# A decoder layer's attention: the second copy of each projection from the first, one division for both heads of a pair, and the transpose by features moved in the slot

## The chip, the core and the metric

The kernel runs on one core of a Trainium2 chip. The core has a matrix engine (TensorE; PE in the profile, its weight loads PEld), VectorE (DVE), ScalarE (ACT), GpSimd (POOL) and SyncE (SP), which here only issues DMAs. The engines run side by side, each through its own queue of instructions in order, and wait for one another by semaphores. Products land in PSUM, which has eight banks of 128 x 512 fp32; everything else lies in SBUF.

The metric is the time of one execution on the device in microseconds. Lower is better.

## What is computed

One pre-norm decoder layer on x (4 batches, 1024 rows, 256 features), with 16 heads of 16 features:

```python
x = x + self_attention(layernorm(x))            # windows of 128 rows, each with the window before it, causal
x = x + cross_attention(layernorm(x), ctx)      # 77 keys, a mask over them, biases on q, k, v and the output
x = x + ffn(layernorm(x))                       # fake-quantised, silu(gate) * up, 704 inner features
```

In both attentions a head's output is `softmax(q k^T / 4) v`, with q, k and v from projections of 256 by 256, and the heads' outputs go through one more projection. The change touches how q and k are laid out and how the softmax's division and the turn of its result are done.

## The kernel before

**Stages.** After the loads and the first normalisation comes the attention of all batches in one long loop, and then the feed-forward part. The mask's rows are compared on the device; here they are alike, so `attention(True)` runs, in which `alike` is true and `queue_of[0]` is SyncE's DMA queue.

**Jobs, units, slots.** The attention has eight jobs in this order: S0, S1, S2, X0, S3, X1, X2, X3 (S self, X cross, and the batch). The 16 heads are in two groups g of eight. A group's projection gives 128 rows: four slots of 32 rows (j), each with two heads of 16 features, parity o = 0 and o = 1. Scores are taken for all j of one (job, g, o) at once, each j in its own strip of 32 rows of TensorE. A unit is (job, g, o, u); u goes over four quarters of the rows in S and two halves in X. There are 96 units, and slots go over them in order. In a slot, work is issued in this order, for every engine alike:

1. the values of a half that has come ready: `weighted_values`, `normalise`, `by_features` (L1239 to L1243; later in the last job's tail);
2. tasks by due time, among them `project` (q or k, by halves of the rows), `values`, `normed_T`, `out_project` and the preparation of the weights; then lighter work beside (statistics, quantisation);
3. `put_maxima`, if a (job, g, o) has all its maxima;
4. `maxima` of the unit five slots ahead (`LEAD` = 5): score products sc_n with queries on the partitions, and on VectorE the row maxima out of PSUM, with the causal mask added (L757) or without (L768);
5. `weights` of this unit: score products sc_t with keys on the partitions, and ScalarE's exp (L822, L844), in S also GpSimd's causal select (L826).

**How one head of two is picked.** `project` (L344) makes both heads' rows of a group in one bank ps_p, and ScalarE reads that bank twice, once for each parity, into two tiles q[g, 0] and q[g, 1] (or k): with `rows[o]`, a column of ones and zeros, as scale, the other head's 16 rows become zero. Of these zero rows one carries the softmax's shift: `put_maxima` (L776) turns the maxima by TensorE, ScalarE copies them (mxT), and four DMAs of SyncE write their negatives into row (1 - o) * 16 of every slot of q; k has a one in that row, from the bias `onerow[o]` (L369). Thus sc_t comes out with the maximum subtracted. In X one more row carries the mask: kx has the mask's row there and q a one, by the bias tile bq_p (`nextrow`, L363). q[g, o] and k[g, o] are eight buffers in turn (`qks`).

**Banks.** All PSUM tiles are whole banks of one pool of eight, given out in turn. A slot takes four for sc_n, four for sc_t and one for every task or value in it. A bank can be written again once the engine that reads it has.

**After the weights.** `weighted_values` (L847) multiplies the weights with the values for one (job, g, o, half) into ps_av, the sum of the weights beside them in column 16; VectorE transposes the bank by blocks of 32 (L880) into o_sb. `normalise` (L882) takes the reciprocal of the sums (L888) and multiplies (L890) into aN, one parity at a time. With o = 1 done, `by_features` (L897) transposes aN back (L902) into aT, from which `out_project` (L904) reads. A half's `out_project` may start in the slot after its last values (`task(end, ...)`, L1201).

Of the kernel before, what the change touches and what calls it, by code (L numbers as in the profile page):

```python
# [25 lines left out]
def decoder_layer(  # L26
# [175 lines left out]
    with ExitStack() as att:  # L202
# [13 lines left out]

        rows, qrows, onerow, nextrow = [], [], [], []
        for o in range(NS):
# [3 lines left out]
            for dst, first, n in (  # L222
# [15 lines left out]
                nc.vector.tensor_reduce(dst, at, AX.XY, ALU.max)  # L238
            q = wp.tile([P, 1], F32, name=f"qrows{o}")
            nc.vector.tensor_scalar(q, m, QSCALE, None, ALU.mult)  # L240
            rows.append(m)
            qrows.append(q)
            onerow.append(w)
            nextrow.append(n2)


        f = stage.tile([P, P], F32, name="cb_f", tag="stage")
        nc.gpsimd.memset(f, 0.0)
# [35 lines left out]
        class Job:  # L284


            def __init__(self, kind, b):
                self.kind, self.b = kind, b
                self.leads = (kind, b) == ("S", 0)
                self.st = {}  # L290
                self.xn, self.xnT, self.vs, self.q, self.k = {}, {}, {}, {}, {}
                self.aN, self.aT, self.mx, self.pts, self.av = {}, {}, {}, {}, {}

            def branch(self):
# [49 lines left out]
        def project(job, g, which, hf):  # L344

            out = job.q if which == "q" else job.k
            w = job.wq if job.kind == "X" else (wq_s if which == "q" else wk_s)
            if hf == 0:
                for o in range(NS):
                    out[g, o] = next_of("qk", qks)  # L350
            ps = bank("ps_p")
            for c in range(NC):
                by_columns(
                    ps,
                    w[:, c, g * P : (g + 1) * P],
                    job.xnT[hf][:, c, :],
                    start=(c == 0),
                    stop=(c == NC - 1),
                )
            for o in range(NS):  # L360
                dst = out[g, o][:, hf * HS : (hf + 1) * HS]
                if job.kind == "X":
                    nc.scalar.activation(  # L363
                        dst, ps, AF.Identity, bias=job.bq[:, g, o : o + 1], scale=qrows[o]
                    )
                elif which == "q":
                    nc.scalar.activation(dst, ps, AF.Copy, scale=qrows[o])  # L367
                else:
                    nc.scalar.activation(dst, ps, AF.Identity, bias=onerow[o], scale=rows[o])  # L369

# [41 lines left out]
        def attention(alike):  # L412
# [16 lines left out]
            vx = wp.tile([SK, B, H + 1, HD + 1], F32, name="vx")  # L429
            bq_p = wp.tile([P, NP, NS], F32, name="bq_p")  # L430
            bk_p = wp.tile([P, NP, NS], F32, name="bk_p")
# [7 lines left out]
            def prep_cross():  # L439
# [12 lines left out]
                def biases():  # L452
                    for name, dst, by, plus in (("q", bq_p, qrows, nextrow), ("k", bk_p, rows, onerow)):
                        for o in range(NS):
                            nc.vector.tensor_scalar(dst[:, :, o], raws[name], by[o], None, ALU.mult)
                            nc.vector.tensor_scalar(
                                dst[:, :, o], dst[:, :, o], plus[o], None, ALU.add
                            )

# [256 lines left out]
            def maxima(job, g, o, u):  # L716
# [33 lines left out]
                for j in range(NJ):  # L750
                    if job.kind == "S":

                        for i in range(2):
                            t = 2 * u + i
                            n = 2 * P if t else P
                            junk = work.tile([P, 2 * P], BF16, name="junk", tag="junk", bufs=2)
                            nc.vector.tensor_tensor_reduce(  # L757
# [18 lines left out]
            def put_maxima(job, g, o):  # L776
# [5 lines left out]
                mxT = work.tile([NJ * NT, P], F32, name="mxT", tag="mxT", bufs=2)  # L782
                nc.scalar.copy(mxT, ps[: NJ * NT, :P])
                for j in range(NJ):
                    row = j * SL + (1 - o) * HD
# [15 lines left out]
            def weights(job, g, o, u):  # L801
# [34 lines left out]
                else:  # L836
# [5 lines left out]
                    for j in range(NJ):  # L842
                        pt = work.tile([SK, HS], F32, name="ptx", tag="pt", bufs=16)
                        nc.scalar.activation(pt, banks[j][:SK], AF.Exp)  # L844
                        job.pts[g, o, j, u] = pt

            def weighted_values(job, g, o, hf):  # L847
                ps = bank("ps_av")
# [25 lines left out]
                if job is jobs[-1] and (g, o, hf) == (NP - 1, NS - 1, NH - 1):  # L874
                    job.av[g, o, hf] = next_of("xnT", xnTs)[
                        :, 0, :
                    ]
                else:
                    job.av[g, o, hf] = work.tile([P, HS], F32, name="o_sb", tag="o_sb", bufs=1)
                nc.vector.transpose(job.av[g, o, hf], ps)  # L880

            def normalise(job, g, o, hf, tail):  # L882

                if o == 0:
                    job.aN[g, hf] = work.tile([P, HS], F32, name="aN", tag="aN", bufs=2)
                on = job.av[g, o, hf].rearrange("p (s e) -> p s e", e=SL)
# [5 lines left out]
                    on[:, :, 0:HD],  # L892
                    rec.to_broadcast([P, HS // SL, HD]),
                    ALU.mult,
                )
# [320 lines left out]
            for slot in range(first, last):  # L1216
# [21 lines left out]
                else:  # L1238
                    for args in values_of.get(slot, ()):  # L1239
                        weighted_values(*args)  # L1240
                        normalise(*args, tail)
                        if not tail:
# [25 lines left out]
                if now:  # L1268
                    if alike or not (ahead and now[0].kind == "X"):
                        weight_bias(*now)  # L1270
                    weights(*now)
                for fn, args in late.get(slot, ()):
                    fn(*args)
# [321 lines left out]
```

## Time and profile before

| | us |
|---|---|
| median of three runs (663.86 to 665.63) | 664.09 |
| the profiled execution, whole | 664.85 |
| its span, first to last instruction | 663.1 |
| attention loop in that span, about | 30 to 545 |
| TensorE, VectorE, ScalarE, GpSimd busy | 613.6, 542.9, 367.9, 269.7 |

The granted TensorE clock averages 0.990 over the span. The page of the profile gives busy time by engine, the chain of work that ended last, and the costliest groups of instructions; a group's line reads: source line, engine, operation, what it writes <- what it reads, shapes, count | busy us, mean ns of one | idle time of the engine before it and what ended it. A timeline row is start, length, engine, line, operation and count, and in brackets the idle time before it. Where ScalarE reads a bank twice in a row, one timeline row with x2 holds both.

### The profile page before, as it was taken

The numbers are of one execution on the slowest core, as the hardware profiler recorded it, in microseconds if no ns is written. First come the engines' busy times: TensorE is split into PE (matmuls) and PEld (weight loads), VectorE is DVE, ScalarE is ACT, GpSimd is POOL, SyncE is SP. The second block draws the span as 40 slices with busy tenths as digits, with TensorE's granted clock in tenths as the row PEclk, the third lists the DMA queues.
The fourth block names the chain that finished last, engine by engine and source line by source line (L and its number), as shares of the span: only waits on it lengthen the run. The fifth ranks groups of instructions, "written<-read, shape, count | busy, mean of one in ns | idle before, by whom it ended". The sixth has DMA issues, their size and how long they took to land.

```text
span 663.1 us, 20225 instructions
## 1 busy us (share of the span) xinstructions
PE 613.6 (93%) x7862; PEld 350.8 (53%) x7862; DVE 542.9 (82%) x1922; ACT 367.9 (55%) x672; POOL 269.7 (41%) x520
## 2 busy tenths in 40 slices
PE   9899899999999999999999999999999997887775
PEld 6456565566555665654456656544444345333564
DVE  6878878768779799678997997897878787789896
ACT  2365564644555534655564456447465565788392
POOL 3164533637234567640054878436601141111032
PEclk9999999999999999999999999999999999989899
DMA  8100100000000000000000000000000110000057
GB/s 290 48 4 15 38 3 3 19 4 6 17 28 11 11 10 11 13 11 19 3 10 11 12 24 26 4 3 4 3 2 4 38 62 17 1 0 1 1 95 164
DMA packets 18078, 17.42 MB, mean 26 GB/s; under 512 B 2998, under 2 KB 17335, under 8 KB 17975
## 3 DMA queue, kind: packets, MB, share of 16 engines
q1 hardware_dynamic: 15783, 14.21, 6.7%
q0 software_dynamic: 1904, 1.84, 2.2%
q8 instruction: 64, 1.05, 0.6%
q14 instruction: 39, 0.32, 0.1%
q10 hardware_dynamic: 288, 0.00, 0.0%
HBM read 9.47 MB, written 6.03 MB: 23 GB/s over the span
## 4 chain that ended last, share of the span: by engine, by line
PE 61%; DVE 26%; ACT 6%; issue 5%; POOL 1%; DVEq 0%; ACTq 0%
PE ps_p L304 13%; PE ps_av L856 7%; PE sc_t L812 7%; PE sc_n L727 6%; PE ps_op L304 6%; PE ps_av L866 4%; DVE junk L757 4%; PE sc_t L841 3%; PE ps_v L304 3%; PE sc_n L742 3%; DVE bnst L192 2%; DVE o_sb L880 2%; PE pg L1393 2%; ACT shared L369 2%; PE ps_idle L117 2%
## 5 line engine op out<-in xcount | busy, mean ns | idle before, releaser
L757 DVE CUSTOM_DVE_ANT_0 junk<-sc_n,cboth 128x256 bf16<-128x256 f32 (+1 forms) x512 | 172.3, 403 | 35.1 <-PE sc_n L727 35.0
L822 ACT ACTIVATE pt<-sc_t 128x512 f32<-128x512 f32 (+1 forms) x256 | 125.4, 576 | 84.9 <-PE sc_t L812 84.9
L826 POOL TENSOR_SCALAR_AFFINE_SELECT pt<-pt 128x256 f32<-128x256 f32 x256 | 102.6, 409 | 114.9 <-ACT pt L822 104.7
L812 PE MATMUL sc_t<-shared 32*128 32x256 f32 (+1 forms) x1024 | 87.1, 375 | 1.4 <-DVE vx L532 0.3
L844 ACT ACTIVATE ptx<-sc_t 77x512 f32<-77x512 f32 x128 | 65.3, 597 | 37.0 <-PE sc_t L841 37.0
L727 PE MATMUL sc_n<-shared 32*128 32x256 f32 (+1 forms) x1024 | 73.6, 387 | 2.9 <-ACT shared L369 1.6
L812 PEld LDWEIGHTS sc_t<-shared 32*128 32x128 f32 x1024 | 65.0, 184 | 13.6 <-ACT shared L367 3.2
L320 POOL TENSOR_SCALAR xn<-x,mv,rs 128x256 f32<-128x256 f32 x56 | 69.9, 1254 | 0.0
L160 POOL TENSOR_SCALAR ve<-mv 128x4 f32<-128x4 f32 x20 | 4.7, 234 | 153.3 <-DVE mv L194 153.2
L880 DVE STREAM_TRANSPOSE o_sb<-ps_av 128x512 f32<-128x512 f32 x63 | 45.0, 714 | 23.8 <-PE ps_av L856 13.7
L304 PE MATMUL ps_p<-shared,w_s 128*32 128x512 f32 x512 | 60.9, 595 | 3.0 <-DVE mx L757 1.4
L727 PEld LDWEIGHTS sc_n<-shared 32*128 32x128 f32 x1024 | 45.7, 184 | 32.2 <-DVE mx L757 10.8
L856 PE MATMUL ps_av<-pt,vt 128*32 128x256 f32 (+1 forms) x1152 | 58.6, 346 | 3.9 <-DVE mx L757 3.6
L768 DVE TENSOR_REDUCE mx<-sc_n 128x4 f32<-128x308 f32 x128 | 51.9, 468 | 8.5 <-PE sc_n L742 8.3
L856 PEld LDWEIGHTS ps_av<-pt,vt 128*32 128x32 f32 x1152 | 34.7, 109 | 31.5 <-DVE mx L757 6.4
L841 PE MATMUL sc_t<-shared,kx 32*77 32x512 f32 x256 | 45.9, 599 | 0.0
L757 DVE DVE_READ_ACCUMULATOR2_ANT mx<- 128x1 f32 x512 | 42.6, 83 | 0.1
L866 PE MATMUL ps_av<-ptx,vx 77*32 77x512 f32 x256 | 36.0, 605 | 3.4 <-DVE mx L768 2.5
L363 ACT ACTIVATE shared<-ps_p,bq_p,qrows 128x512 f32<-128x512 f32 x32 | 23.2, 774 | 26.0 <-PE ps_p L304 26.0
L742 PEld LDWEIGHTS sc_n<-kx,shared 32*128 32x128 f32 x1024 | 31.7, 186 | 10.2 <-DVE rec L888 1.7
L742 PE MATMUL sc_n<-kx,shared 32*128 32x77 f32 x1024 | 36.5, 277 | 0.0
L1408 ACT ACTIVATE act<-pg,gsc 128x512 f32<-128x512 f32 x44 | 29.2, 687 | 12.5 <-PE pg L1393 9.9
(201 smaller groups left out, 989.0 us busy)
## 6 DMA issues: line engine op xcount, KB each, us to landing
x<-in_x_dram SPq DMA_DIRECT2D x8, 512.0 KB
out_dram<-shared SPq DMA_DIRECT2D x9, 256.0 KB
shared<-mxT SPq DMA_DIRECT2D x128, 4.0 KB
out_dram<-x SPq DMA_DIRECT2D x7, 256.0 KB
out_dram<-shared POOLq DMA_DIRECT2D x7, 256.0 KB, 4.7
w_s<-in_L_attn_w_qkv_dram SPq DMA_DIRECT2D x2, 384.0 KB
raw_d<-in_L_ffn_w_down_dram SPq DMA_DIRECT2D x2, 352.0 KB
raw_f<-in_L_ffn_w_gate_dram SPq DMA_DIRECT2D x5, 128.0 KB
```

The source lines that it names most:

```text
L304: nc.tensor.matmul(out[r], lhsT[:, r], rhs, skip_group_check=True, **on)
L320: eng.tensor_scalar(xn, xb[job.b][:, t, :], job.st[hf].mv[:, i, 0:1], job.st[hf].rs[:, i : i + 1], ALU.subtract, ALU.mult,)
L727: nc.tensor.matmul(banks[j][:, (i + 1) * 2 * P - n : (i + 1) * 2 * P], q[r, t * P : (t + 1) * P], k[r, k0 * P : k0 * P + n], start=True, s ...
L742: nc.tensor.matmul(banks[j][:, i * SK : (i + 1) * SK], q[r, t * P : (t + 1) * P], k[r, :], start=alike, stop=alike or i == HT - 1,)
L757: nc.vector.tensor_tensor_reduce(out=junk[:, 2 * P - n :], in0=banks[j][:, (i + 1) * 2 * P - n : (i + 1) * 2 * P], in1=cboth[:, 2 * P - n ...
L812: nc.tensor.matmul(banks[j][:, w : w + n], k[r, t * P : (t + 1) * P], q[r, t * P : t * P + n], start=True, stop=True,)
L822: nc.scalar.activation(pt.rearrange("p i a q -> p (i a q)")[:, :w], banks[j][:, :w], AF.Exp)
L826: nc.gpsimd.affine_select(out=pt[:, :, 0, :], in_=pt[:, :, 0, :], compare_op=ALU.is_ge, fill=0.0, base=0, pattern=[[0, 2], [1, P]], channe ...
L841: nc.tensor.matmul(banks[j][:SK], k[r, :], q[r, s], start=alike, stop=True)
L844: nc.scalar.activation(pt, banks[j][:SK], AF.Exp)
L856: nc.tensor.matmul(ps[j * SL : (j + 1) * SL, (a0 - t0) * P : (a1 - t0) * P], slot_of(job.vs[kb // 2][:, kb % 2], heads[j]), job.pts[g, o, ...
L866: nc.tensor.matmul(ps[j * SL : (j + 1) * SL, :], slot_of(vx[:, job.b], heads[j]), job.pts[g, o, j, hf], start=True, stop=True,)
```

## The change

Three things change.

`project` reads the bank once. Of the two tiles the first written holds both heads' rows: q[g, 1] and k[g, 0]. The other, q[g, 0] or k[g, 1], is written from it in SBUF, with the rows of the other head made zero. Of a pair q[g, o], k[g, o] one side is thus still zero in the other head's rows. The row of ones that `onerow` gave k in S is now written by one DMA in `put_maxima`, ahead of the four of the maxima. In X two DMAs after each projection write the zeros and ones into two rows of every slot of q[g, 1]. `qrows` falls away, `none_one` comes, and the biases need fewer instructions.

`normalise_pair` does the division for both parities at once, for all jobs but the last: the two transposed banks lie in one tile of two halves (`pair`).

It and `by_features` are issued at the end of the slot, after `maxima` and `weights`, while `weighted_values` with its transpose stays first. The buffers' counts change: o_sb is twice as wide and has two, aN one, junk one.

```diff
@@ -236,14 +236,16 @@
                     channel_multiplier=1,
                 )
                 nc.vector.tensor_reduce(dst, at, AX.XY, ALU.max)
-            q = wp.tile([P, 1], F32, name=f"qrows{o}")
-            nc.vector.tensor_scalar(q, m, QSCALE, None, ALU.mult)
             rows.append(m)
-            qrows.append(q)
             onerow.append(w)
             nextrow.append(n2)
 
 
+        none_one = []
+        for row in range(2):
+            t = wp.tile([NJ, P], F32, name=f"fill{row}")
+            nc.gpsimd.memset(t, float(row))
+            none_one.append(t)
         f = stage.tile([P, P], F32, name="cb_f", tag="stage")
         nc.gpsimd.memset(f, 0.0)
         nc.gpsimd.affine_select(
...
@@ -357,16 +360,23 @@
                     start=(c == 0),
                     stop=(c == NC - 1),
                 )
-            for o in range(NS):
-                dst = out[g, o][:, hf * HS : (hf + 1) * HS]
-                if job.kind == "X":
-                    nc.scalar.activation(
-                        dst, ps, AF.Identity, bias=job.bq[:, g, o : o + 1], scale=qrows[o]
+            half = [out[g, o][:, hf * HS : (hf + 1) * HS] for o in range(NS)]
+            if job.kind == "X":
+                nc.scalar.activation(
+                    half[1], ps, AF.Identity, bias=job.bq[:, g : g + 1], scale=QSCALE
+                )
+                nc.scalar.activation(
+                    half[0], half[1], AF.Identity, bias=nextrow[0], scale=rows[0]
+                )
+                for row in range(2):
+                    queue_of[0].dma_start(
+                        out=half[1][row : P : SL, :].rearrange("j (t q) -> j t q", q=P),
+                        in_=none_one[row].unsqueeze(1).to_broadcast([NJ, HT, P]),
                     )
-                elif which == "q":
-                    nc.scalar.activation(dst, ps, AF.Copy, scale=qrows[o])
-                else:
-                    nc.scalar.activation(dst, ps, AF.Identity, bias=onerow[o], scale=rows[o])
+                return
+            first = 1 if which == "q" else 0
+            nc.scalar.activation(half[first], ps, AF.Copy, scale=QSCALE if which == "q" else 1.0)
+            nc.scalar.activation(half[1 - first], half[first], AF.Copy, scale=rows[1 - first])
 
 
         leading = Job("S", 0)
...
@@ -427,7 +437,7 @@
             wo_x = wp.tile([P, NC, D], F32, name="wo_x")
             kx = wp.tile([P, NP, NS, B * SK], F32, name="kx")
             vx = wp.tile([SK, B, H + 1, HD + 1], F32, name="vx")
-            bq_p = wp.tile([P, NP, NS], F32, name="bq_p")
+            bq_p = wp.tile([P, NP], F32, name="bq_p")
             bk_p = wp.tile([P, NP, NS], F32, name="bk_p")
             bv_b = wp.tile([SK, D], F32, name="bv_b")
             bo_b = wp.tile([P, D], F32, name="bo_b")
...
@@ -450,12 +460,11 @@
                     queue_of[0].dma_start(out=bo_b, in_=bo.partition_broadcast(P))
 
                 def biases():
-                    for name, dst, by, plus in (("q", bq_p, qrows, nextrow), ("k", bk_p, rows, onerow)):
-                        for o in range(NS):
-                            nc.vector.tensor_scalar(dst[:, :, o], raws[name], by[o], None, ALU.mult)
-                            nc.vector.tensor_scalar(
-                                dst[:, :, o], dst[:, :, o], plus[o], None, ALU.add
-                            )
+                    nc.vector.tensor_scalar(bq_p, raws["q"], QSCALE, None, ALU.mult)
+                    for o in range(NS):
+                        nc.vector.tensor_scalar(
+                            bk_p[:, :, o], raws["k"], rows[o], onerow[o], ALU.mult, ALU.add
+                        )
 
                 def transposed(w, name, dst=None):
                     def load():
...
@@ -753,7 +762,7 @@
                         for i in range(2):
                             t = 2 * u + i
                             n = 2 * P if t else P
-                            junk = work.tile([P, 2 * P], BF16, name="junk", tag="junk", bufs=2)
+                            junk = work.tile([P, 2 * P], BF16, name="junk", tag="junk", bufs=1)
                             nc.vector.tensor_tensor_reduce(
                                 out=junk[:, 2 * P - n :],
                                 in0=banks[j][:, (i + 1) * 2 * P - n : (i + 1) * 2 * P],
...
@@ -781,6 +790,13 @@
                 )
                 mxT = work.tile([NJ * NT, P], F32, name="mxT", tag="mxT", bufs=2)
                 nc.scalar.copy(mxT, ps[: NJ * NT, :P])
+                if job.kind == "S":
+                    queue_of[0].dma_start(
+                        out=job.k[g, o][(1 - o) * HD : P : SL, :].rearrange(
+                            "j (t q) -> j t q", q=P
+                        ),
+                        in_=none_one[1].unsqueeze(1).to_broadcast([NJ, NT, P]),
+                    )
                 for j in range(NJ):
                     row = j * SL + (1 - o) * HD
                     queue_of[0].dma_start(
...
@@ -844,6 +860,9 @@
                         nc.scalar.activation(pt, banks[j][:SK], AF.Exp)
                         job.pts[g, o, j, u] = pt
 
+            def apart(job):
+                return job is jobs[-1] or not alike
+
             def weighted_values(job, g, o, hf):
                 ps = bank("ps_av")
                 heads = [2 * NJ * g + 2 * j + o for j in range(NJ)]
...
@@ -875,14 +894,23 @@
                     job.av[g, o, hf] = next_of("xnT", xnTs)[
                         :, 0, :
                     ]
+                elif not alike:
+                    job.av[g, o, hf] = work.tile([P, HS], F32, name="o_sb", tag="o_sb", bufs=1)
                 else:
-                    job.av[g, o, hf] = work.tile([P, HS], F32, name="o_sb", tag="o_sb", bufs=1)
+                    if o == 0:
+                        job.pair[g, hf] = work.tile(
+                            [P, NS, HS], F32, name="o_sb", tag="o_sb", bufs=2
+                        )
+                    job.av[g, o, hf] = job.pair[g, hf][:, 0 if apart(job) else o, :]
                 nc.vector.transpose(job.av[g, o, hf], ps)
 
             def normalise(job, g, o, hf, tail):
 
                 if o == 0:
-                    job.aN[g, hf] = work.tile([P, HS], F32, name="aN", tag="aN", bufs=2)
+                    if alike:
+                        job.aN[g, hf] = job.pair[g, hf][:, 1, :]
+                    else:
+                        job.aN[g, hf] = work.tile([P, HS], F32, name="aN", tag="aN", bufs=2)
                 on = job.av[g, o, hf].rearrange("p (s e) -> p s e", e=SL)
                 rec = small.tile([P, HS // SL, 1], F32, name="rec")
                 nc.vector.reciprocal(rec, on[:, :, HD : HD + 1])
...
@@ -891,6 +919,19 @@
                     aN[:, :, o * HD : (o + 1) * HD],
                     on[:, :, 0:HD],
                     rec.to_broadcast([P, HS // SL, HD]),
+                    ALU.mult,
+                )
+
+            def normalise_pair(job, g, hf):
+
+                aN = job.aN[g, hf] = work.tile([P, HS], F32, name="aN", tag="aN", bufs=1)
+                on = job.pair[g, hf].rearrange("p o (s e) -> p o s e", e=SL)
+                rec = small.tile([P, NS, HS // SL, 1], F32, name="rec2")
+                nc.vector.reciprocal(rec, on[:, :, :, HD : HD + 1])
+                nc.vector.tensor_tensor(
+                    aN.rearrange("p (s o d) -> p o s d", o=NS, d=HD),
+                    on[:, :, :, 0:HD],
+                    rec.to_broadcast([P, NS, HS // SL, HD]),
                     ALU.mult,
                 )
...
@@ -1238,6 +1279,8 @@
                 else:
                     for args in values_of.get(slot, ()):
                         weighted_values(*args)
+                        if not apart(args[0]):
+                            continue
                         normalise(*args, tail)
                         if not tail:
                             by_features(*args)
...
@@ -1269,6 +1312,10 @@
                     if alike or not (ahead and now[0].kind == "X"):
                         weight_bias(*now)
                     weights(*now)
+                for job, g, o, hf in values_of.get(slot, ()):
+                    if o == NS - 1 and not apart(job):
+                        normalise_pair(job, g, hf)
+                        by_features(job, g, o, hf)
                 for fn, args in late.get(slot, ()):
                     fn(*args)
                 while after:
```

## The prediction

> **What bounds the kernel now.** I read the times by stage first, then the chain that ended last, the instruction groups, the list of waits, and the timeline and the DMA queue around the edited lines.
>
> The stages (start:end, length, then busy time and count for PE, PEld, DVE, ACT, POOL; granted clock; DMA share; GB/s):
>
> ```profile
> 30.00:300.00 270.00, 259.37 (x3735) 156.33 (x3735) 215.16 (x973) 145.32 (x283) 139.58 (x281) 1.00 0.05 13
> 300.00:545.00 245.00, 238.52 (x3241) 122.46 (x3238) 207.12 (x691) 137.69 (x274) 102.14 (x191) 1.00 0.05 15
> ```
>
> Both attention stretches are TensorE's: 497.9 us busy of 515, at clock 1.00; VectorE is second with 80% and 85%. So VectorE's time is worth something only where it makes TensorE wait. The feed-forward after 556 us is not touched. On the page the chain says the same: PE 61%, DVE 26%, ACT 6%.
>
> But a busy PE is not a PE at its peak. Look at one slot of the timeline (start, length, engine, instruction):
>
> ```profile
> 120.23 1.90 PE L304 MATMUL ps_p<-shared,w_s 128*32 128x512 f32 x16
> 120.53 0.72 DVE L880 STREAM_TRANSPOSE o_sb<-ps_av 128x512 f32<-128x512 f32 x1 [0.59 <-PE ps_av L856]
> 122.03 0.71 DVE L902 STREAM_TRANSPOSE aT<-aN 128x512 f32<-128x512 f32 x1
> 122.25 1.45 ACT L369 ACTIVATE shared<-ps_p,onerow,rows 128x512 f32<-128x512 f32 x2 [1.96 <-PE ps_p L304]
> 123.03 1.85 PE L812 MATMUL sc_t<-shared 32*128 32x256 f32 x16
> 123.23 0.42 DVE L757 CUSTOM_DVE_ANT_0 junk<-sc_n,cboth 128x256 bf16<-128x256 f32 x1 [0.48 <-PE sc_n L727]
> 135.41 0.88 PE L812 MATMUL sc_t<-shared 32*128 32x256 f32 x16
> ```
>
> There are eight banks in one rotation. A slot takes one for its projection and eight for its scores, so the ninth, the last of sc_t, is the projection's own, and sc_t stands until ScalarE has read it twice (until 123.70). The same 16 matmuls take 0.88 us at 135.41 and 1.85 here. Over the kernel, idle weight loading in front of sc_t on those reads (us, times; from the views of L812 and L841):
>
> ```profile
>   ACT shared L367: 3.2, 10
>   ACT shared L369: 2.9, 6
>   ACT shared L363: 2.5, 7
>   ACT shared L363: 3.1, 7
>   ACT shared L367: 0.7, 2
> ```
>
> That is 12.4 us in 32 waits, 0.39 each.
>
> **Part 1, the bank read once.** There are 48 projections, 16 each of self q, self k and cross q. The first read now has an immediate scale: ScalarE's PSUM copies of 128x512 without operand tiles take 0.594 (L341) and 0.602 (L822). Cross q keeps a bias tile: a scale tile alone makes 0.684 (L367), so I take 0.70. A bank was held for 1.27 (two L367, which overlap), 1.45 (L369) or 1.45 us (L363); it will be for 0.60, 0.60 or 0.70. Each hold is 0.67 to 0.85 shorter, more than the mean wait of 0.39, so nearly all the 12.4 us can go. Behind them stands the next user's bank, which waits for VectorE's maxima: at 124.81 that bank was free from 123.93, so there 0.8 us is won in full. I take 80%, **-10 us** (ends 0 and -12.4). The second write now reads SBUF and depends on the first: 0.70 for q and k and 0.79 for cross q, from L941's 128x256 Abs rows (0.513 out of SBUF) against L1053's (0.492 out of PSUM). The halves are thus complete 1.33 to 1.52 us after the product, against 1.27 to 1.45: nothing, since ScalarE is 55% busy and the half that the next maxima take is early.
>
> A rule speaks against this: the Trainium skill, "VectorE: DVE Perf Modes", section "The TRN2 errata — SBUF-src ops pay a fixed extra latency per instruction", gives ScalarE 224 cycles from SBUF against 172 from PSUM. By it 48 reads would cost 48 x 43 ns = 2.1 us more ScalarE time, by L941 and L1053 1.0 us; both lie off the path.
>
> **Part 2, VectorE.** 28 pairs (seven jobs, two groups, two halves; the last job keeps the old form). Each had two reciprocals (L888, 0.253) and two products (L890, 0.425): 1.36 us. A pair has one of each at twice the width: reciprocals of 1 and 16 columns take 0.164 and 0.253, so 32 take 0.35, and L1523's 512-wide product 0.69: 1.04. That saves 0.32 x 28 = 8.9 us of VectorE, and 0.68 us (o=0) or 1.39 us (o=1) leaves the place ahead of the slot's maxima. This counts only where VectorE does not wait for the scores anyway: of 96 units' maxima 42 do (34 waits of junk on sc_n, 8 of mx), as at 123.23 above, where the moved work had filled idle time. Slot by slot I took the smaller of two: the moved work that really delays the maxima, and what TensorE lost behind these maxima, against the shortest run of the same matmuls. The sum is 17 us. Against it, 1.75 us (0.35 + 0.69 + 0.71) now follow the maxima of each o=1 slot and can make the next slot's late: at 84.65 the maxima end and the next begin at 85.56, so they would be 0.85 late; at 128.41 some 0.1. Taking 0.47 for the 16 self pairs: 7.5 us. The net is **-7 us** if 85% of the 17 comes true (ends -17 and +7). The junk buffer's one copy fewer is nothing: VectorE writes it in its own order.
>
> **Part 3, the transpose by features comes later than its reader.** An output projection may start one slot after. Of 14 (job, half) cases, four start so early that the new order is late:
>
> ```profile
> 507.40 0.71 DVE L902 STREAM_TRANSPOSE aT<-aN 128x512 f32<-128x512 f32 x1
> 508.04 1.35 DVE L951 TENSOR_REDUCE big<-far 128x1 f32<-128x256 f32 x4
> 509.58 1.63 DVE L768 TENSOR_REDUCE mx<-sc_n 128x4 f32<-128x308 f32 x4
> 510.10 1.93 PE L304 MATMUL ps_op<-wo_x,aT 128*32 128x256 f32 x32
> ```
>
> Here aT was ready at 508.1 and ps_op began at 510.10. Now big and maxima run to about 510.3 and the 1.75 us to 512.0: 1.9 us of TensorE. Likewise at 416.45 (2.0), 466.81 (1.1) and 516.07 (1.0); in the others at least 2.5 us are left. Queued behind the waiting product are that slot's scores. **+6 us** (ends 0 and +8).
>
> **Part 4, rows by DMA.** 16 issues for self keys (32 pieces) and 32 for cross q (16 pieces) join SyncE's queue. One issue holds it 0.63 us (L786; L554's 16 pieces 0.55). The self one waits only for the last sc_n, four to six us before mxT, and stands ahead of it while SyncE waits for mxT anyway (368 us in all): nothing, unless that cover goes. Cross q's rows are read two slots later. But in two slots they stand ahead of a tight burst:
>
> ```profile
> 265.21 1.45 ACT L363 ACTIVATE shared<-ps_p,bq_p,qrows 128x512 f32<-128x512 f32 x2 [1.70 <-PE ps_p L304]
> 266.81 2.79 SPq L786 DMA_DIRECT2D shared<-mxT  x4
> 270.49 1.81 PE L812 MATMUL sc_t<-shared 32*128 32x256 f32 x16
> ```
>
> The rows issue after the second read (266.7), two of 0.65, then the keys' one: the burst begins some 1.9 us late and ends at 271.5; its last packet moves about 0.75 after the issue (the first burst: 34.55 and 35.29). The fourth row is wanted near 270.9. So 1.5 us here and at 398.63: **+3 us** (ends 0 and +7, if all 16 bursts came 0.65 late: in eight the slack is under 0.65, by 3.4 us in sum).
>
> A rule sets it higher: "DMA: Bandwidth & Descriptors", section "Anatomy of one DMA — SWDGE (gpsimd) path", puts some 2.0 us on every transfer, for another queue than this; with it in place of 0.63 + 0.75 the two places would cost 1.2 us more together.
>
> TensorE also waits for one more semaphore per (group, parity): 32 at 0.051 (the EVENT_SEMAPHORE of L812), **+1 us** with its lag. The start (two fewer VectorE operations, two more memsets) and the biases are under 0.5 us: nothing.
>
> **Sum:** -10 - 7 + 6 + 3 + 1 = -7 against the profiled 664.85 us (span 663.1 and 1.75 around it): 657.9; the median of the three runs is 0.76 lower, so **657 us**.
>
> **The rivals.**
> *A, both covers come through.* The 12.4 and the 17 us are won whole and the late transposes cost what is above: -12.4 - 17 + 10 = -19, **645**. For it: 60 us of weight-load waits name L757 or L768. Against: each us that TensorE gains brings VectorE, at 85%, nearer to its bound.
> *B, slower: maxima pushed by what now follows them.* If every pair makes the next slot's maxima 0.85 late, 28 x 0.85 = 24, with +10 for the rest, against -10 and -17: +7, **671**. It decides from 0.6 us per pair ((10 + 17 - 10) / 28). For it: in 42 units the old place was free time, which now stays empty. Against: many slots are 5 to 7 us long, and maxima with the pair take 4.6.
> *C, it hardly shows.* The bank's gain is used up by parts 3 and 4 and VectorE's order nets zero: **664**. For it: the waits on L363 to L369 are 0.4 us each, and the next bank's may take their place.
>
> **Chances.** Forecast 0.43 (650 to 662), A 0.22, C 0.12 (within 2 us of before, the 0.3% that a measurement of this kernel can tell from no change), B 0.23. So faster 0.65, same 0.12, slower 0.23. The range 643 to 669 leaves out the far ends of A and B, some 0.2; the forecast's own is 650 to 662.
>
> **What would show it.** Right: sc_t's waits on the projection's reads under 3 us in sum, no 1.85 us sc_t; L880 followed at once by maxima; reciprocals at 0.35 x 28. Wrong: ps_op idle before aT in more than four places (part 3), sc_t waiting on mxT's rows in more than two slots (part 4), or TensorE's waits on L757 not smaller than before (part 2, rival B).

## The result, and the profile after

The changed kernel takes **723.07 us** (median of 6 runs, 721.27 to 726.69) against 664.78 for the kernel before on the same chip (663.62 to 665.63): ratio 1.0886, 95% interval [1.0866, 1.0906]. It is 58 us slower; the forecast was 657, 8 us faster. The profiled execution's span is 720.4 us (663.1 before).

The stretches of the profile after that answer to the two attention stages shown of before (same columns; the attention now ends near 590):

```profile
30.00:300.00 270.00, 241.97 (x3238) 143.02 (x3229) 213.09 (x896) 125.27 (x245) 122.09 (x248) 0.96 0.04 11
300.00:590.00 290.00, 272.03 (x3707) 137.74 (x3703) 223.95 (x689) 149.31 (x295) 113.29 (x208) 0.96 0.05 14
```

In the same 270 us TensorE gets 3238 matmuls done where it did 3735, is busy for 242 instead of 259 us, and is granted 0.96 of its clock instead of 1.00. VectorE is no busier in a stretch, but needs more of them. The chain of work that ended last, as shares of the span by engine:

```profile
PE 52%; DVE 34%; ACT 6%; issue 5%; POOL 1%; DMA 1%; DVEq 0%; ACTq 0%
```

Before, VectorE had 26% of it. TensorE's waits for VectorE stand in the list of waits of the kernel after (who <- whom, us, times, longest):

```profile
PEld sc_n L736 <- DVE mx L766: 32.9, 49, 0.9
```

Before, the same wait was:

```profile
PEld sc_n L727 <- DVE mx L757: 10.8, 20, 0.8
```

So the maxima come late. Their own rows, in the groups kept apart by shape, first of the kernel before, then of the kernel after:

```profile
L757 DVE CUSTOM_DVE_ANT_0 junk<-sc_n,cboth 128x256 bf16<-128x256 f32 x448 | 162.5, 420 | 23.9 <-PE sc_n L727 23.9
```

```profile
L766 DVE CUSTOM_DVE_ANT_0 junk<-sc_n,cboth 128x256 bf16<-128x256 f32 x448 | 189.6, 423 | 48.3 <-PE sc_n L736 17.2 <-PE ps_p L307 0.5 <-PE ps_av L875 0.5
```

The same 448 instructions of the same 0.42 us occupy 189.6 instead of 162.5 us (their records no longer overlap), and of the idle time before them, 48.3 us, only 17.2 are a wait for the scores; before, all was. The timelines say how that can be. Before:

```profile
123.23 0.42 DVE L757 CUSTOM_DVE_ANT_0 junk<-sc_n,cboth 128x256 bf16<-128x256 f32 x1 [0.48 <-PE sc_n L727]
123.58 0.42 DVE L757 CUSTOM_DVE_ANT_0 junk<-sc_n,cboth 128x256 bf16<-128x256 f32 x1
```

After:

```profile
30.32 0.42 DVE L766 CUSTOM_DVE_ANT_0 junk<-sc_n,cboth 128x256 bf16<-128x256 f32 x1
...
30.90 0.42 DVE L766 CUSTOM_DVE_ANT_0 junk<-sc_n,cboth 128x256 bf16<-128x256 f32 x1
...
31.37 0.42 DVE L766 CUSTOM_DVE_ANT_0 junk<-sc_n,cboth 128x256 bf16<-128x256 f32 x1
...
34.98 0.28 PE L788 MATMUL ps_mx<-ident,mx 128*32 128x128 f32 x1 [3.62 <-DVE mx L766]
```

Before, one 128x256 maxima starts 0.345 us after the last, while the tail of that one's record still runs. After, the next starts 0.47 us later within a bank (30.90 to 31.37) and 0.58 us later from one bank to the next (30.32 to 30.90): the medians are 0.467 and 0.576. At 31 us TensorE has nothing else and stands 3.62 us until the maxima are there.

### The profile page after: what moved, and what is told of

The parts are those of the page before. It is cut to its first block, busy times and chain, and to the rows that moved or that the text cites. A ratio compares the mean times of both kernels' runs of the same rounds, so it can differ in the third digit from the quotient of the medians.

```text
span 720.4 us, 20139 instructions
## 1 busy us (share of the span) xinstructions
PE 641.5 (89%) x7862; PEld 358.9 (50%) x7862; DVE 567.7 (79%) x1859; ACT 368.0 (51%) x672; POOL 270.6 (38%) x522
## 4 chain that ended last, share of the span: by engine, by line
PE 52%; DVE 34%; ACT 6%; issue 5%; POOL 1%; DMA 1%; DVEq 0%; ACTq 0%
DVE junk L766 13%; PE ps_p L307 9%; PE ps_av L875 7%; PE sc_n L736 6%; PE sc_t L828 6%; PE ps_op L307 6%; PE ps_av L885 3%; PE sc_n L751 3%; PE ps_v L307 2%; PE sc_t L857 2%; PE ps_idle L117 2%; DVE bnst L192 2%; DVE aT L943 2%; DVE aN L931 2%; DVE mx L777 2%
## 5 line engine op out<-in xcount | busy, mean ns | idle before, releaser
L766 DVE CUSTOM_DVE_ANT_0 junk<-sc_n,cboth 128x256 bf16<-128x256 f32 (+1 forms) x512 | 208.1, 406 | 69.1 <-PE sc_n L736 31.0
L736 PE MATMUL sc_n<-shared 32*128 32x256 f32 (+1 forms) x1024 | 89.1, 400 | 11.0 <-DVE mx L766 9.0
L828 PE MATMUL sc_t<-shared 32*128 32x256 f32 (+1 forms) x1024 | 93.4, 388 | 5.2 <-DVE x L961 1.5
L828 PEld LDWEIGHTS sc_t<-shared 32*128 32x128 f32 x1024 | 71.0, 194 | 16.7 <-ACT mxT L792 2.7
L736 PEld LDWEIGHTS sc_n<-shared 32*128 32x128 f32 x1024 | 52.6, 188 | 48.2 <-DVE mx L766 32.9
L875 PE MATMUL ps_av<-pt,vt 128*32 128x256 f32 (+1 forms) x1152 | 63.4, 366 | 8.9 <-DVE mx L766 5.8
L307 PE MATMUL ps_p<-shared,w_s 128*32 128x512 f32 x512 | 62.4, 608 | 3.0 <-DVE mx L766 2.0
L378 ACT ACTIVATE shared<-ps_p 128x512 f32<-128x512 f32 x32 | 19.1, 597 | 50.7 <-PE ps_p L307 50.7
L307 PE MATMUL ps_op<-wo_s,aT 128*32 128x256 f32 x512 | 32.3, 392 | 3.3 <-DVE aT L943 1.6
```

What stands on the lines that cost most here:

```text
L307: nc.tensor.matmul(out[r], lhsT[:, r], rhs, skip_group_check=True, **on)
L736: nc.tensor.matmul(banks[j][:, (i + 1) * 2 * P - n : (i + 1) * 2 * P], q[r, t * P : (t + 1) * P], k[r, k0 * P : k0 * P + n], start=True, s ...
L766: nc.vector.tensor_tensor_reduce(out=junk[:, 2 * P - n :], in0=banks[j][:, (i + 1) * 2 * P - n : (i + 1) * 2 * P], in1=cboth[:, 2 * P - n ...
L828: nc.tensor.matmul(banks[j][:, w : w + n], k[r, t * P : (t + 1) * P], q[r, t * P : t * P + n], start=True, stop=True,)
L875: nc.tensor.matmul(ps[j * SL : (j + 1) * SL, (a0 - t0) * P : (a1 - t0) * P], slot_of(job.vs[kb // 2][:, kb % 2], heads[j]), job.pts[g, o, ...
```

## The experiments

Times are medians; the kernel before ran beside each, at 664.5 to 664.9 us.

### The two junk buffers, given back and taken away

`e1_after_junk2`: the changed kernel with two junk buffers; to make room in SBUF the row of zeros for the DMAs comes from a tile of zeros that is there already.

```diff
-t = wp.tile([NJ, P], F32, name=f"fill{row}")
...
+none_one += [zeros[0:NJ].bitcast(F32), t]
...
-junk = work.tile([P, 2 * P], BF16, name="junk", tag="junk", bufs=1)
+junk = work.tile([P, 2 * P], BF16, name="junk", tag="junk", bufs=2)
```

> The changed kernel with two junk buffers again as before (to make room, the DMA of zeros reads the existing tile of zeros; nothing else differs). Theory J (one junk buffer makes each masked maximum wait for the end of the one before it; start to start 0.468 us within a bank and 0.576 us across banks, where before it was 0.345): the maxima start every 0.345 us again, the half-clock dips in the attention vanish, and the time falls from 723 to 650 to 664 us. Theory O (the pair's division and the transpose by features, now behind the maxima, hold up the output projections and the next slot): the pace returns but the time stays over 690 us. Theory R (the rows that the DMAs write are late): over 690 us as well, with sc_t waiting on mxT's rows.

680.92 us (679.89 to 685.56), ratio 1.024 [1.0217, 1.0263]: 42 us come back, and the maxima start every 0.345 us again (median). But the time stays 16 us over the kernel before and above theory J's 664, and the granted clock is still at 0.5 for 31 us of the attention (44 in the kernel after), in the profiled execution, the longest of its five. It is below what O and R expected. The runs after e9 take up what stays.

`e2_before_junk1`: the kernel before with that one number changed, 2 to 1.

> The kernel before with one junk buffer and nothing else changed. Theory J: 448 maxima of 256 columns and 64 of 128 lose 0.12 us (second of a bank) or 0.23 us (first of a bank), 0.12 x 256 + 0.23 x 256 = 90 us of VectorE's time, of which the idle time before maxima hides a part: 705 to 740 us, pace 0.468 and 0.576. Theories O and R: within 2 us of 664.5.

707.86 us (706.4 to 708.92), ratio 1.0638 [1.0613, 1.0664]: **+43 us from one number**. Its group of maxima is that of the kernel after:

```profile
L757 DVE CUSTOM_DVE_ANT_0 junk<-sc_n,cboth 128x256 bf16<-128x256 f32 x448 | 189.5, 423 | 40.4 <-PE sc_n L727 10.2
```

The size follows from this row: the group takes 27.0 us more, and of the 40.4 us before it 30.2 are no wait for scores (none before), so 57.2; the 128x128 ones lose 7.1 more by the same reckoning. Of these 64 us, 17.3 lie in time in which VectorE had waited for scores (34.9 us of it, now 17.6). The other 47 are near the 43 measured.

`e9_one_junk_two_halves`: one buffer again, twice as wide, its halves in turn.

```diff
+if job.kind == "S":
+    both = work.tile([P, 4 * P], BF16, name="junk", tag="junk", bufs=1)
...
-junk = work.tile([P, 2 * P], BF16, name="junk", tag="junk", bufs=2)
+junk = both[:, 2 * P * i : 2 * P * (i + 1)]
```

> The kernel before with one junk buffer of twice the width; the first maxima of each bank write its left half, the second ones its right half, so that no two in a row write the same bytes. Theory (what costs the 43 us is the wait of a maxima for the one just ahead of it, because both write the same bytes): the same as before within 0.5%, 662 to 668, start to start 345 ns. Rival (what costs is that one buffer is given out anew for every instruction, or that a single buffer stands for all, whatever the bytes): slower by several per cent, 690 to 708, as with one narrow buffer.

664.85 us (663.74 to 666.67), ratio 1.0001 [0.9987, 1.0016], and the maxima start every 0.345 us:

```profile
L759 DVE CUSTOM_DVE_ANT_0 junk<-sc_n,cboth 128x256 bf16<-128x256 f32 x448 | 162.5, 419 | 24.0 <-PE sc_n L727 23.7
```

So it is the bytes and not the number of buffers. The programs as built show the wait that they bring. One and the same instruction, the second maxima of a bank, first with two buffers and then with one narrow one:

```
L757 ISA junk,mx<-sc_n,cboth 128x256 [waits DVE_49 >= 77]
L757 ISA junk,mx<-sc_n,cboth 128x256 [waits DVE_49 >= 78]
```

DVE_49 is VectorE's own semaphore, and the maxima just ahead brings it to 78. With two buffers the instruction thus waits for the maxima before the last (206 of the 256 second maxima do, the other 50 wait for none on VectorE), which is over by then. With one narrow buffer all 256 wait until the last one has not only been issued but finished, because they write the same bytes, which nobody reads. The Trainium skill, "VectorE: DVE Perf Modes", section "The DRAIN you can't avoid", reports that a semaphore after each of eight copies cost nothing extra. Here that holds for a wait on the maxima before the last, at 0.345 us from start to start; a wait on the last one costs 0.12 and 0.23 us each. The measurement decides.

### The bank read once, alone

`e3_bank_once` has the edits of `project`, `put_maxima` and the biases and nothing else.

> The kernel before with only the projection's part (bank read once, rows written by DMA, fewer bias instructions); two junk buffers, division by head and transpose in the old place. Prediction's terms: -10 for the bank, +3 for two late bursts of rows, +1 for semaphores: 658 us, range 652 to 664. Theory R: over 680 us.

662.33 us (660.94 to 664.25), ratio 0.9961 [0.9948, 0.9974]: -2.5 us. Its timeline at the place that the prediction named:

```profile
261.80 0.56 SPq L793 DMA_DIRECT2D shared<-fill  x1
262.45 2.75 SPq L801 DMA_DIRECT2D shared<-mxT  x4
265.29 0.77 PEld L827 LDWEIGHTS sc_t<-shared 32*128 32x128 f32 x6 [1.36 <-ACT shared L367]
265.32 3.21 PE L827 MATMUL sc_t<-shared 32*128 32x256 f32 x16 [1.24 <-DMA shared<-mxT]
```

mxT was there at 260.2, but two cross rows, a load of weights and the keys' row (fill, 261.80) go first, and the burst of its four DMAs begins at 262.45. sc_t waits 1.24 us for these rows, and then its 16 matmuls take 3.21 us: the last ten wait until 266.5 and run at a granted clock of 0.5, which lasts for 6.8 us from 266.4. `e7_bank_rows_after` changes only the place of the cross rows' DMAs: they go into a list that is emptied at the slot's end, behind those of `put_maxima`.

```diff
+fills = []
...
+def fill():
     for row in range(2):
         queue_of[0].dma_start(
...
+fills.append(fill)
...
+while fills:
+    fills.pop(0)()
```

> The projection's part alone as in the run before, but the cross rows' two DMAs are issued at the end of the slot, behind the four of the maxima. Theory S (the two late bursts of rows and the stretch at half clock after the first took the bank's gain): sc_t waits on mxT's rows no more, no half clock near 266 us, 655 to 660 us. Rival T (the bank's gain was never more than 2 to 3 us, since the next bank's wait takes its place): 661 to 664 us.

**657.43 us** (654.17 to 658.45), ratio 0.9873 [0.985, 0.9896]: -7.4 us, and so 4.9 us were the DMAs' place: the burst above now begins at 260.36, with mxT. Theory S is met; one stretch of 3.4 us at half clock is left in the attention, at 280.2. The groups of sc_t (idle time at the end of the line, by what ended it):

```profile
L832 PE MATMUL sc_t<-shared 32*128 32x256 f32 (+1 forms) x1024 | 76.8, 368 | 1.0 <-ACT mxT L796 0.3 <-DVE vx L545 0.3 <-DVE kx L523 0.3
L832 PEld LDWEIGHTS sc_t<-shared 32*128 32x128 f32 x1024 | 60.4, 185 | 7.6 <-ACT mxT L796 2.7 <-DVE vx L545 0.7 <-DVE kx L523 0.7
```

Of the waits for a projection's reads one of 0.4 us is left (12.4 us in 32 before), and none for a DMA; sc_t, 87.1 us busy before, takes 76.8.

### The pair and its place

`e4_pair_late` has `normalise_pair` with its buffers and the late place for it and `by_features`, but neither the bank nor the junk.

> The kernel before with only the pair's division and the later transpose; two junk buffers, banks read twice. Prediction's terms: -7 for VectorE, +6 for four late output projections: 663.5 us, range 655 to 675. Theory O: over 690 us.

682.83 us (680.43 to 683.69), ratio 1.0262 [1.0238, 1.0285]: +18.0, outside the range and short of theory O. `e5_pair_early` has the pair's division and the transpose where they had been, both in the slot of o = 1 ahead of its maxima.

```diff
+if not apart(args[0]):
+    if args[2] == NS - 1:
+        normalise_pair(args[0], args[1], args[3])
+        by_features(*args)
+    continue
```

> The kernel before with the division once for both heads and by_features in the old place, ahead of the slot's tasks and maxima; nothing moved. Theory P (the 18 us of the pair's part come from the late place): faster than before by some of the 8.9 us of VectorE's time saved: 656 to 664 us. Theory Q (the pair itself costs, since all the division of two heads now falls into one slot): 668 to 680 us.

668.49 us (667.46 to 670.42), ratio 1.0061 [1.0039, 1.0082]. So the pair by itself is +3.6, though VectorE is busy 9 us less (533.7 against 542.9), and the place is +14.3. `e6_pair_late_op_later` is e4 with `task(end + 1, ...)` in place of `task(end, ...)` for `out_project`, so that no output projection comes ahead of its aT.

> The pair's part alone, late as in the change, but an output projection may start one slot later than there. Theory H1 (the late transpose costs through the output projections that wait for aT: three waits of 2 us, two of them followed by stretches at half clock): 666 to 673 us, no ps_op wait on aT. Theory H3 (it costs through the banks that VectorE empties late in the following slot, x of the output projection and the copies of the transposed input, for which sc_t stands): over 677 us.

674.06 us (672.96 to 674.35), ratio 1.0133 [1.0109, 1.0157]: 8.8 us of the place go with output projections that come before their aT. In e4 there are three:

```profile
PEld ps_op L305 <- DVE aT L928: 5.0, 3, 2.1
```

The clock is at 0.5 from the end of one of these waits and from the start of another. But e6 lets every output projection start a slot later, and that alone was not run on the kernel before. 5.5 us stay, between the two expectations. The timeline of e4 shows what else is late:

```profile
161.09 0.35 DVE L915 RECIPROCAL rec<-o_sb 128x32 f32<-128x32 f32 x1
161.47 0.69 DVE L916 TENSOR_TENSOR aN<-o_sb,rec 128x512 f32<-128x512 f32 x1
162.19 0.71 DVE L928 STREAM_TRANSPOSE aT<-aN 128x512 f32<-128x512 f32 x1
162.83 0.65 DVE L946 TENSOR_TENSOR x<-x,ps_op 128x512 f32<-128x512 f32 x1
...
163.53 1.13 PE L813 MATMUL sc_t<-shared 32*128 32x256 f32 x10 [0.64 <-DVE x L946]
```

ps_op had been written by 161.3. VectorE empties that bank (L946) behind the pair's 1.75 us, and sc_t, whose turn it is to have the bank, stands until then; weight loading for it stood 1.04 us. This is not the next maxima being late, but a bank that a task in the slot leaves for VectorE to read. In sum over the attention, weight loads wait no longer for x than before (4.4 us, 4.3 before). Beside those for aT, the waits that grew most are for other banks that VectorE empties, into the copies of the transposed input (4.3 us, none before) and into o_sb (8.2, 1.8). Those for aN fell (1.8, 14.6).

Which of the three late instructions costs was taken apart further. `e10_turn_late`: the kernel before, division by parity in place, only the transpose moved.

```diff
-if not tail:
+if not tail and args[0] is jobs[-1]:
     by_features(*args)
...
 weights(*now)
+for args in values_of.get(slot, ()):
+    if args[0] is not jobs[-1]:
+        by_features(*args)
```

> The kernel before with the transpose by features alone moved behind the slot's maxima and weights; the divisions by parity stay where they were, two junk buffers. With pair and late place together the time was 682.8, with the pair in the old place 668.5. Theory (the late place costs through aT for the output projection, which depends on the transpose alone, and through the next banks that VectorE empties): the transpose is 0.71 of the 1.75 us that were moved, so aT comes 1.04 earlier than there and most of the cost goes: 666 to 672. Rival (it is the place of aT alone, whatever stands before it, that costs): the whole of the late place's 14 us, 677 to 681.

663.43 us (661.98 to 665.77), ratio 0.9982 [0.9966, 0.9998]: it costs nothing, less than either expectation. `e11_pair_early_turn_late` is e5 with this move:

> The kernel before with the pair's one division in the old place and the transpose by features alone behind the slot's maxima and weights; two junk buffers. Measured so far: the pair and the transpose in the old place 668.5, both late 682.8, the transpose alone late (division by parity) 663.4. Theory (it is the division standing late, 1.04 of the 1.75 us, that makes the late place cost; the transpose may stand late for nothing): 665 to 670. Rival (with the pair's division any lateness of the transpose costs most of the 14 us, since aT then follows 1.75 us of work that has bunched in one slot): 676 to 683.

660.29 us (659.12 to 661.46), ratio 0.9932 [0.991, 0.9955]: better than either expectation, and 22.5 us better than with the division late too. `e13_reciprocal_early` is e4 with the reciprocal alone (0.35 of the 1.75 us) back in the old place:

```diff
+def reciprocal_pair(job, g, hf):
+    on = job.pair[g, hf].rearrange("p o (s e) -> p o s e", e=SL)
+    rec = job.pair[g, hf, "rec"] = small.tile([P, NS, HS // SL, 1], F32, name="rec2")
+    nc.vector.reciprocal(rec, on[:, :, :, HD : HD + 1])
```

> The kernel before with the pair's form, its reciprocal (0.35) in the old place, its product (0.69) and the transpose (0.71) behind the slot's maxima and weights: 1.40 us late instead of 1.75 (682.8 us) or 0.71 (660.3 us). Theory (what stands late pushes the next slot's reads of banks and maxima one for one in the slots where VectorE has no slack, so the cost grows with its length): between the two by length, 660.3 + 22.5 x 0.69 / 1.04 = 675, within 671 to 679. Rival (the late place costs only in the few slots that a longer lateness pushes over an edge, or costs as soon as any of the division stands there): near one of the ends, 660 to 666 or 681 to 685.

669.62 us (669.36 to 669.79), ratio 1.0074 [1.0055, 1.0092]: below what was expected, but between the ends. The waits of VectorE for the scores, in e11, e13 and e4, with 0.71, 1.40 and 1.75 us late:

```profile
DVE junk L758 <- PE sc_n L728: 39.2, 31, 3.7
```

```profile
DVE junk L758 <- PE sc_n L728: 45.3, 36, 3.7
```

```profile
DVE junk L758 <- PE sc_n L728: 49.4, 34, 3.8
```

What leaves the old place leaves idle time there, 6 and 10 us of it, and stands behind the maxima instead. With it grow sc_t's idle weight loads (12.9, 15.8, 19.2 us) and the time at half clock in the attention (0, 3.4, 20.5 us). If a stretch at clock 0.5 loses half its length (an estimate), 1.7 of the 9.3 us and 10.2 of the 22.5 are the clock's; the other 7.6 and 12.3 stand as 1 to 1.6, near the 0.69 to 1.04 us of late division (1 to 1.5). That the cost grows with the length of the late division fits this, but three runs do not show it slot by slot.

### The parts that pay, together

`e8_bank_rows_after_pair_early` is e7 with e5's pair (e8 and e14 take the row of zeros as e1 does).

> The projection's part with its rows at the end of the slot, and the pair's division in the old place, with two junk buffers. If the gains add up: the gain of the pair in the old place plus that of the projection's part, 645 to 658 us. If both gains are the same waits of TensorE: no better than the better of the two.

657.96 us (657.29 to 658.94), ratio 0.9895 [0.9875, 0.9915]: no better than e7. `e12_bank_rows_after_turn_late` is e7 with e10's late transpose:

> The kernel before with the bank read once, the cross rows' DMAs behind the maxima's, and the transpose by features late; division by parity, two junk buffers. Theory: the two effects measured apart, -7.4 and -1.1 us, add up: 654 to 658, at or a little under the 657.4 of the first alone. Rival: the transpose's microsecond was the scatter between runs, or its lateness costs once TensorE has the bank's time back: 657 to 661.

654.56 us (652.79 to 656.2), ratio 0.9843 [0.9814, 0.9871]. `e14_all_three` is e7 with e11's pair and late transpose: the whole change but for the place of the division, the place of the cross rows' DMAs and the junk.

> All of the change with three things altered: two junk buffers, the cross rows' DMAs behind the maxima's, and the pair's division in the old place (the transpose stays late). Theory: the effects measured apart add up, -7.4 for the bank and -4.6 for pair and transpose: 650 to 655. Rival (they want the same idle time, as the pair in the old place did with the bank, 658.0 for 657.4 + 3.6): 654 to 659, no better than with division by parity, 654.6.

**650.57 us** (650.43 to 651.36), ratio 0.9789 [0.977, 0.9808], the fastest kernel here: 14 us under the kernel before.

## Why the prediction was wrong

The parts, run alone as e3, e4 and e2, add up to the whole:

| | predicted | measured |
|---|---|---|
| bank read once with its DMAs (parts 1 and 4) | -6 | -2.5 (e3) |
| pair and order on VectorE (part 2) | -7 | +9.2 (18.0 in e4, less 8.8 by e6) |
| output projections behind the late transpose (part 3) | +6 | +8.8 (e4 less e6) |
| one junk buffer (part 2, last sentence) | 0 | +43.1 (e2) |
| sum | -7 | +58.6; the whole measured +58.3 |

The split of e4's 18.0 us between the second and the third row rests on e6 and is an estimate; their sum is not.

**The step that failed** is the last sentence of part 2: "The junk buffer's one copy fewer is nothing: VectorE writes it in its own order." The order is indeed VectorE's own, but writing in order is not the same as writing without a wait. With the same bytes the next maxima waits for the end of the last one, and 0.345 us becomes 0.47 or 0.58. That is 43 of the 66 us between forecast and result. In the trace of before the sign was there to be read: maxima of 0.42 us that start every 0.345 overlap, and an overlap is what a shared output takes away. The range had no room for it since the edit was costed at nothing instead of being bounded.

**Part 2's order**, the next largest miss, 16 us. The durations were right: the reciprocal of 32 columns, forecast 0.35, takes 0.346, the product, forecast 0.69, 0.713 in the changed kernel:

```profile
L931 DVE TENSOR_TENSOR aN<-o_sb,rec 128x512 f32<-128x512 f32 x28 | 20.0, 713 | 1.0
L930 DVE RECIPROCAL rec<-o_sb 128x32 f32<-128x32 f32 x28 | 9.7, 346 | 0.0
```

What failed are both halves of "-17 and +7.5". The 17 us were the time that earlier maxima should give TensorE; but in e4 its weight loads of sc_n wait 10.5 us for the maxima where they had waited 10.8, while VectorE waits for the scores 14 us longer (49.4 for 35.0). So some 14 us of the moved work had filled idle time, and TensorE's waits for the maxima hardly fell (over all its weight loads in the attention, 67.5 us for 69.7). And the 7.5 us were the next slot's late maxima, without the banks that VectorE empties for sc_t and without the clock. The part that was costed as one move is two: the transpose may go late (-1.1 alone, -8.2 with the pair), the division may not (+22.5). That the pair ahead of all maxima is +3.6 in spite of 9 us less work may come of its bunching, 2.5 us ahead of one slot's maxima and 0.72 ahead of the other's, where before it was 2.1 and 1.4; that fits e11, where taking 0.71 from the fuller slot gains 8.2, but it wasn't tried by itself.

**Part 3** had the mechanism right, four output projections ahead of their aT (three were seen in e4), and 6 us against 8.8; beside the 5.0 us of waits stands the clock, at half for 20.5 us of the attention in e4 and 13.7 in e6 (half of the difference, 3.4 us, by the estimate above).

**Part 1** was right in its mechanism and near in size. e7 gains 7.4 us with the self keys' DMAs and the semaphore in it, where -10 and +1 had been forecast; the waits on the projection's reads went as said. First reads of 0.60 are 0.597, second reads of 0.70 are 0.722:

```profile
L379 ACT ACTIVATE shared<-shared,rows 128x512 f32<-128x512 f32 x32 | 23.1, 722 | 1.1
L378 ACT ACTIVATE shared<-ps_p 128x512 f32<-128x512 f32 x32 | 19.1, 597 | 50.7 <-PE ps_p L307 50.7
```

**Part 4** named the place, the burst near 266, and forecast 3 us for the cross rows; it is 4.9 (e3 less e7), within its bounds, and again the clock is in the difference (6.8 us at half in e3, 3.4 in e7).

**The rivals.** B had the sign, and its price for work that stands behind the maxima, 24 us, is near the 22.5 that the late division costs. That is luck: its mechanism was late maxima, and in e4 TensorE's waits for them did not grow. It said 671 because it set the 17 us against this price. Without the junk the change is 680.9 (e1), and B would have been the nearest. A and C fell. None of the three had the cause of the greater part.

## What to carry to other kernels

A scratch output that nobody reads is still a dependency: on one in-order engine, here VectorE, two instructions in a row that write the same bytes ran one after the other, so give such an output two places, in one buffer or in two, and count a cut from two to one as a new wait on every instruction. Before moving work behind a slot's urgent instructions, look at whether the engine had been idle in the old place, and at every bank that it must empty next in the new one. In a queue, DMAs that are read two slots later go behind those that are read in this slot.

## What the runs showed of the hardware

In the attention the granted TensorE clock falls to 0.5 for 3.4 us or a multiple: not at all in before, e5, e8, e9 and e11, for 3.4 us in e7, e10, e13 and e14, 6.8 in e3 and e12, 13.7 in e6, 20.5 in e2 and e4, 31 in e1 and 44 in the kernel after. One such place in the kernel after (start:end, length, busy time of PE, PEld, DVE, ACT, POOL, granted clock, DMA share, GB/s):

```profile
31.50:35.00 3.50, 0.02 (x1) 0.02 (x1) 2.96 (x15) 0.59 (x1) 0.00 (x0) 1.00 0.00 0
35.00:35.80 0.80, 0.80 (x17) 0.61 (x17) 0.80 (x4) 0.26 (x1) 0.00 (x0) 1.00 0.00 0
35.80:39.20 3.40, 3.40 (x24) 0.59 (x16) 2.34 (x14) 0.00 (x0) 0.00 (x0) 0.50 0.02 5
39.20:42.60 3.40, 3.29 (x48) 1.88 (x48) 3.14 (x16) 2.34 (x5) 1.62 (x3) 1.00 0.02 5
```

TensorE waits 3.5 us for the maxima, works for 0.8, and then runs 3.4 us at half clock: the 16 matmuls of a projection take 3.36 us there (36.27 in the timeline), and 1.90 in the kernel before (120.23). So this wait was paid once by itself and once more behind it. The Trainium skill, "TensorE: Matmul & The Clock Gate", section "What's actually happening", tells of a half-rate state after an idle window of some 3.4 us. This place agrees; but the nine others in the attention of the kernel after followed pauses of only 0.4 to 1.5 us, in 3.4 us in which TensorE was busy for 44 to 78%. The busy share alone doesn't decide it: the kernel before was busy for 61% in the 3.4 us from 284.0 and kept its clock. What does decide it was not tried.
